# Where buffers lie and where small sums run in an attention and feed-forward kernel: a change of placement in the second half

## The chip, the cores and the metric

The kernel runs on one core of one Trainium2 chip. The metric is the device time of one execution in microseconds (us). The kernel before takes 2131.32 us, the median of three runs (2130.99 to 2131.37).

A core has a matrix engine (PE; its weight loads are listed apart as PEld), a vector engine (DVE), an activation engine (ACT), GpSimd (POOL) and a queue (SP) that issues most of the DMAs. Each engine works through its own list in the order in which the program gives it. PE writes to PSUM; DVE and ACT read PSUM; POOL works on SBUF alone.

## The reference

Eight sequences of 512 rows and 512 columns pass through attention and then a feed-forward block. Everything is in fp32.

```python
x = x + layernorm(attention(layernorm(x)))          # 16 heads of 32, rotary on all of q and k
h = layernorm(x)
h = fwht(h * SU_ug) / SCALE                          # Walsh-Hadamard over 512
up   = h @ W_up.T   * (Wscale_ug[:2048] * SCALE)     # 512 -> 2048
gate = h @ W_gate.T * (Wscale_ug[2048:] * SCALE)
h = fwht(silu(gate) * up * SU_dp) / SCALE            # Walsh-Hadamard over 2048
h = h @ W_down.T * (Wscale_dp * SCALE)               # 2048 -> 512
out = x + layernorm(h)
```

## The kernel before

**Two halves.** Up to about 916 us the program does attention for the eight sequences and stores the rows of `x + layernorm(attention)` to DRAM (`x1d`). From there on it does the feed-forward block. The change is in the second half alone.

**The end of attention.** The last sequence's four tiles of 128 rows are normed by DVE (line 955), added to the input rows by POOL (956) and stored by DMAs that POOL issues (957). They lie in four buffers `y` of the attention's pools. The feed-forward pools `fw` and `fs` are laid over the attention's pools. A tile tag gets its place when it is first asked for, in that order: `tt_room` and `pr_room` at lines 1053 and 1054 fix the places of `tt` (8 buffers of 3584 bytes in each partition) and `pr` (6 of 4096); then come `sig` and the `g` tiles. The first writer of a tile waits for the last users of what lay there.

**Pairs and features.** The sequences are taken in four pairs p (bA = 2p, bB = 2p + 1). The 2048 features are 16 blocks of 128; i runs over 8, and block i goes with block i + 8. For one i, the 2 x 2 problem (two feature blocks, two halves of the input columns, two sequences) is done by Strassen's scheme: seven products in the order 1, 2, 6, 5, 7, 3, 4, on sums of weights and of operands, joined by additions.

**The first pair** (p = 0, to about 1180 us; `seven`, line 1149): each i has a gate unit ("g") and an up unit ("u"), so 16 units u = 0 to 15. A product is two matmuls over 512 columns, in one of four PSUM buffers that go round (`ubank`). Product 1 is copied to SBUF by ACT (m1); DVE adds it to product 2 (c11, line 1170), to product 6 (u2, 1172), then 7, 3 and 4; ACT copies product 5 (m5, 1174); POOL makes c22 and c12 (1177, 1180). `catch_up` runs three scalings or activations of the unit before. `middle` runs the input steps below, `filler` runs down matmuls. `hook(n)` is called after the step of product n. Weights' sums over two blocks of the first pair's unit are made by POOL for the next unit at a unit's start (`combine`, 144) and, over gate and up, by DVE into four tiles w2 (`deep_weights`, lines 1018 to 1021); `deep_keep` writes all to DRAM for the later pairs. `load_unit` loads weights two units ahead.

**The deep pairs** (p = 1, 2, 3; `pair`, line 1311, and `deep`, 1098): gate and up are joined by a second Strassen level. Each of the seven products n is now seven small products m in the order 1, 2, 6, 5, 7, 3, 4 over 256 columns, each in one `ubank`. ACT copies small products 1 (line 1115) and 5 (1119), DVE does the five additions 1116, 1118, 1122, 1124 and 1127, POOL two (1123, 1125) and the additions between products (1320). After m = 2, 5 and 3 `deep` calls `place(1)`, `place(2)` and `place(3)`, and `copied` after the copy of small product 5: other work is hung in there, named (n, at). `part()` runs one down matmul (two instructions of 512 columns).

**The operands of a pair** are sums of quarters of the Hadamard-transformed inputs `xb`: `operand` (T1 to T4, line 230, 1024 columns), `deep_operand` (three sums of 256 columns for each n into a `tt` tile, line 1005), and `deep_last` (one in place, line 1010, needed by small product 7 of that n). `prepare` (line 1279) has a table of which is made at which (i, n, at).

**Input steps.** Each 128-row tile of the next pair is loaded (`in_load`), its statistics taken (`in_stats`: DVE and two small POOL instructions), its shift made (`in_shift`, DVE), normed (`in_norm`, ACT), transposed (`in_flip`) and Hadamard-transformed (`in_had`). `FIRST_CUTS` and `CUTS` say how many steps run in each unit or i.

**Down and end.** Each finished feature block `g` (`scale`, line 1143) is multiplied with four column blocks of the down weights (line 1205) into four PSUM banks. After 16 blocks `finish` scales the four banks into `fy` (1230) and hangs the ends on a list: statistics of four tiles (`norms`), a shift, and `close`, which norms by ACT (1252), adds the residual by POOL and stores. `proceed` runs the next end. All orders are written out by hand (manual schedule).

Of the kernel before, what the change touches and what calls it, by code (L numbers as in the profile page):

```python
# [10 lines left out]
F32 = mybir.dt.float32  # L11
BF16 = mybir.dt.bfloat16
I32 = mybir.dt.int32
AF = mybir.ActivationFunctionType
# [19 lines left out]
def sandwich_kernel(  # L34
# [952 lines left out]
    def tt_tile(name):  # L987
        return fs.tile([P, 7 * P], F32, tag="tt", name=name, bufs=8)
# [1 line left out]
    def pr_tile(name):  # L990
        return fs.tile([P, 2, S], F32, tag="pr", name=name, bufs=6)

    def deep_operand(p, n, k=None):

        if k in (None, 0):
            if n == 4:
                t = xb[2 * p + 1][:, 0:2].rearrange("p k s -> p (k s)")
            else:
                t = tt_tile(f"tt{n}_{p}")
            tt[p, n] = t[:, : 3 * HS].rearrange("p (a s) -> p a s", a=3)  # L1000
        x_, t = ops[p][OPERAND[n]], tt[p, n]
        a, b = [
            (x_[:, 0, HS:], x_[:, 0, :HS]), (x_[:, 1, HS:], t[:, 0]), (x_[:, 1, :HS], t[:, 1]),
        ][k]
        nc.vector.tensor_sub(t[:, k], a, b)
# [6 lines left out]
    def deep_weights(i):  # L1012

        w2[i] = t0, t1, t2, t3 = [
            tt_tile(f"w2_{i}_{k}").rearrange("p (s m) -> p s m", m=P) for k in range(4)
        ]
        wg, wu = wt[0, i, "g"][:, 0:7], wt[0, i, "u"][:, 0:7]
        nc.vector.tensor_add(t0, wu[:, :, 0], wu[:, :, 1])
        nc.vector.tensor_sub(t1, t0, wg[:, :, 0])
        nc.vector.tensor_sub(t2, wg[:, :, 1], t1)  # L1020
        nc.vector.tensor_sub(t3, wg[:, :, 0], wu[:, :, 0])


    INNER = {1: 0, 2: 1, 5: 2, 6: 3, 3: 4, 7: 5, 4: 6}
# [26 lines left out]


    tt_tile("tt_room")
    pr_tile("pr_room")
    psy0 = [ps_y.tile([P, D], F32, tag=f"y{t}", name=f"psy_0_{t}") for t in range(NT)]
    ubank("u0")
# [92 lines left out]
    def seven(p, i, what, filler, middle, hook):  # L1149

        def use(c, b, half):
            f = i + half * NH
            if what == "g":
                gs[b, f] = fs.tile([P, S], F32, tag="sig", name=f"s_{b}_{f}", bufs=4)
                activate(gs[b, f], c, f)
            else:
                scale(b, f, c, gs.pop((b, f)))

        def catch_up():
            while late:
                late.pop(0)()

        bA, bB = 2 * p, 2 * p + 1
        t = [pr_tile(f"pr{what}{k}_{i}") for k in range(4)]
        m1, m5, u2, c11 = t[0][:, 0], t[0][:, 1], t[1][:, 0], t[1][:, 1]
        u3, c22, c12 = t[2][:, 0], t[2][:, 1], t[3][:, 0]
        nc.scalar.copy(m1, product(p, i, what, 1))
        nc.vector.tensor_add(c11, product(p, i, what, 2), m1)  # L1170
        catch_up()
        nc.vector.tensor_add(u2, product(p, i, what, 6), m1)
        use(c11, bA, 0)
        nc.scalar.copy(m5, product(p, i, what, 5))
        hook(5)
        nc.vector.tensor_add(u3, product(p, i, what, 7), u2)
        nc.gpsimd.tensor_add(c22, u3, m5)
        hook(7)
        nc.vector.tensor_add(c12, product(p, i, what, 3), u2)
        nc.gpsimd.tensor_add(c12, c12, m5)  # L1180
        hook(3)
        middle()
        filler()
        nc.vector.tensor_add(u3, product(p, i, what, 4), u3)
        late.extend([lambda: use(c22, bB, 1), lambda: use(c12, bB, 0), lambda: use(u3, bA, 1)])

    psy = {}
# [37 lines left out]
    def finish(b, t, ps):  # L1225
# [15 lines left out]
        def norms(t):  # L1241
            bn(mv[:, t, :], y[:, t], f"o{b}_{t}")
            if t == NT - 1:
                sr.append(inverse_std(mv, NT, f"o{b}"))
                residuals(0)

        def close(t):
            if t == 0:
                sr.append(shift_of(mv, sr[0], NT, f"o{b}"))
            rs, sh = sr  # L1250
            for t in (t, t + 1):
                nc.scalar.activation(
                    y[:, t], y[:, t], AF.Identity, bias=sh[:, t : t + 1], scale=rs[:, t : t + 1]
                )
                nc.gpsimd.tensor_add(y[:, t], r[t], y[:, t])
                nc.sync.dma_start(out=out[b, ts(t, P), :], in_=y[:, t])
            if t == 1:
                residuals(2)

        for t in range(NT):  # L1260
            ends.append(lambda t=t: norms(t))
        for t in (0, 2):
            ends.append(lambda t=t: close(t))

    def proceed():
        if ends:
            ends.pop(0)()

    queue = []

# [8 lines left out]
    def prepare(p, i, n, at):  # L1279
        q = p + 1 if i >= NH - 2 else p  # L1280
        if q >= NP or q == 0:
            return
        todo = {
            (NH - 2, 7, 1): [("ops",), ("tt", 1, 0)], (NH - 2, 7, 2): [("tt", 1, 1)],
            (NH - 2, 7, 3): [("tt", 1, 2)], (NH - 2, 3, 1): [("tt", 2, 0)],
            (NH - 2, 3, 2): [("tt", 2, 1)], (NH - 2, 3, 3): [("tt", 2, 2)],
            (NH - 1, 7, 1): [("T", 0)], (NH - 1, 7, 2): [("T", 1)], (NH - 1, 7, 3): [("last", 1)],
            (NH - 1, 3, 1): [("T", 2)], (NH - 1, 3, 2): [("tt", 6, 0), ("tt", 6, 1)],
            (NH - 1, 3, 3): [("tt", 6, 2)], (NH - 1, 4, 1): [("tt", 5, 0), ("tt", 5, 1)],
            (NH - 1, 4, 2): [("tt", 5, 2), ("tt", 7, 0)], (NH - 1, 4, 3): [("tt", 7, 1), ("tt", 7, 2)],  # L1290
            (0, 1, 1): [("T", 3)], (0, 1, 2): [("last", 2)], (0, 1, 3): [("last", 6)],
            (0, 2, 1): [("tt", 3, 0)], (0, 2, 3): [("tt", 3, 1), ("last", 5)],
            (0, 6, 1): [("tt", 3, 2), ("last", 7)], (0, 6, 2): [("tt", 4, 0)],
            (0, 6, 3): [("tt", 4, 1)], (0, 5, 1): [("tt", 4, 2)], (0, 5, 2): [("last", 3)],
            (0, 5, 3): [("last", 4)],
        }
        for kind, *which in todo.get((i, n, at), ()):
            if kind == "ops":
                ops[q] = {"B11": xb[2 * q][:, 0:2], "B21": xb[2 * q][:, 2:4], "B22": xb[2 * q + 1][:, 2:4]}
            elif kind == "tt":  # L1300
                deep_operand(q, *which)
            elif kind == "T":
                operand(q, *which)
            else:
                deep_last(q, *which)


    PARTS = {1: (1, 3), 2: (1, 3), 6: (1, 2, 3), 5: (1, 3), 7: (1, 3), 3: (1, 2, 3), 4: (1, 3)}
# [2 lines left out]
    def pair(p, i, inputs):  # L1311
# [16 lines left out]
        def copied(n):  # L1328

            if n in (1, 2, 6) and before:  # L1330
                silu(*before[{1: "c22", 2: "c12", 6: "c21"}[n]])
            elif n == 5:
                silu(pr[2], bA, i)

        def place(n, at):
            if at in PARTS[n]:
                part()
            key = n, at
            if late and n in (1, 2) and at == 2:
                while late:  # L1340
                    late.pop(0)()
            elif before and key in ((2, 2), (6, 3), (5, 1)):
                end(*before[{2: "c22", 6: "c12", 5: "c21"}[n]])
            elif key in ((6, 1), (6, 2)):
                nc.vector.tensor_add(pr[2][:, at - 1], pr[2][:, at - 1], pr[1][:, at - 1])
            elif key == (7, 1):
                end(pr[2], bA, i)
            prepare(p, i, n, at)

        for n in ORDER:  # L1350
            now[0] += 1
# [2 lines left out]
                load_two(q // 2 + 2)  # L1354
            if n in (2, 5, 3):
                if inputs:
                    in_step(*inputs.pop(0))
                proceed()
            pr[n] = pr_tile(f"pr{n}_{p}_{i}")
            deep(  # L1360
                p, i, n, pr[n][:, 0], pr[n][:, 1], lambda n=n: copied(n), lambda at, n=n: place(n, at)
            )
            if n == 6:
                add(6, 6, 1)
            elif n == 7:
                add(7, 7, 6)
# [7 lines left out]

    CUTS = [0, 3, 6, 9, 12, 14, 16, 16, 16]
    FIRST_CUTS = [0, 0, 0, 1, 2, 3, 5, 6, 7, 9, 10, 11, 13, 14, 15, 16, 16]
    first = 2 * NT
    for _ in range(3):  # L1380
        wd_load()
    for u, (p, i, what) in enumerate(units):
# [9 lines left out]
            deep_keep(i, what)  # L1392
        steps = [(2 * NT + s // 2, s % 2, len(rows)) for s in range(FIRST_CUTS[u], FIRST_CUTS[u + 1])]

        def middle():
            if u == 1:
                deep_weights(0)
                in_stats(first)
                in_stats(first + 1)
            while steps:  # L1400
                in_step(*steps.pop(0))
            proceed()
            if what == "g" and i > 0:
                deep_weights(i)

        def filler():
            if u >= 2 * NH - 2:
                for at in (1, 2, 3):
                    prepare(0, NH - 2 + u % 2, 3, at)
            down()  # L1410

        def hook(n):
            if u >= 2 * NH - 2 and n == 7:
                for at in (1, 2, 3):
                    prepare(0, NH - 2 + u % 2, 7, at)

        seven(p, i, what, filler, middle, hook)
        if u == 1:
            deep_keep(0, what)
            in_shift(first)  # L1420
            in_shift(first + 1)
            in_norm(first)
        if u == 2 * NH - 1:
            for at in (1, 2, 3):
                prepare(0, NH - 1, 4, at)
        down()
    for p in range(1, NP):
        for i in range(NH):
# [121 lines left out]
```

## Time and profile before

| | |
|---|---|
| median of three runs | 2131.32 us |
| the profiled execution's own time | 2132.84 us |
| its span, first to last instruction | 2131.1 us |
| PE busy | 2087.3 us, 98% |
| DVE, ACT, POOL busy | 1408.7, 744.2, 1567.0 us |
| PE clock granted | 0.995 of full speed |
| DMA | 218 MB, a mean of 102 GB/s |

A profile line of a group or of the timeline names the source line, the engine, the operation, what it writes and reads, its shape and its count; in square brackets stands the idle time of its engine before it and what ended that. A busy PE is not a PE at its peak: the end of a matmul is modelled, so the rate is better read from one start to the next. An fp32 matmul shows as two instructions.

### The profile page before, as it was taken

To read this page: it belongs to the slowest core of one execution; us is meant where nothing else is said; L and a number is where in the kernel's file an instruction comes from. 1 tells how busy PE (TensorE), PEld (TensorE's weight loads), DVE (VectorE), ACT (ScalarE), POOL (GpSimd) and SP (SyncE) were. 2 spreads that over 40 slices of the span, in tenths; PEclk is the share of its full clock that TensorE was granted. 3 is DMA by queue.
4 is the path that set the end of the run, shared out by engine and by line. 5 is a ranking of instruction groups with operands and counts; after the bars stand their busy time and mean duration, and the time that the engine had idled before them with its cause. 6 is when DMAs were issued, how large, how long until landed. Compare 5 with 4: busy or idle time off the path is not lost.

```text
span 2131.1 us, 26822 instructions
## 1 busy us (share of the span) xinstructions
PE 2087.3 (98%) x9035; PEld 1056.8 (50%) x9042; DVE 1408.7 (66%) x2362; ACT 744.2 (35%) x1199; POOL 1567.0 (74%) x1623
## 2 busy tenths in 40 slices
PE   8999999999999999989999999999999999999998
PEld 4333333333333333334444667766666776777663
DVE  5697877676767677355556866668756569556542
ACT  3554545454555555512111132222222221222211
POOL 4787979697978788545554578788787787787862
PEclk9999999999999999999999999999999999999999
DMA  3112121212121122317454444443343343443331
GB/s 120 36 31 51 45 56 41 61 41 55 46 48 54 26 70 74 111 47 220 146 169 151 143 149 138 127 156 122 117 151 125 118 171 123 149 156 132 135 114 69
DMA packets 215914, 218.13 MB, mean 102 GB/s; under 512 B 87376, under 2 KB 147920, under 8 KB 215776
## 3 DMA queue, kind: packets, MB, share of 16 engines
q1 hardware_dynamic: 215424, 215.32, 32.4%
q8 instruction: 72, 1.18, 0.2%
q0 software_dynamic: 352, 1.08, 0.1%
q14 instruction: 66, 0.54, 0.1%
HBM read 169.18 MB, written 46.92 MB: 101 GB/s over the span
## 4 chain that ended last, share of the span: by engine, by line
PE 89%; DVE 6%; issue 2%; POOL 1%; ACT 1%; DMA 0%; POOLq 0%; SPq 0%; DVEq 0%; ACTq 0%
PE d L1108 21%; PE psy L1205 16%; PE s L520 6%; PE ops L599 6%; PE ps_k L432 5%; PE ps_y L655 5%; PE t L566 5%; PE u L1093 4%; PE g L1093 4%; PE psz L1451 3%; PE t L557 2%; PE l L616 2%; PE ps_q L447 1%; PE ps_v L459 1%; PE ps_cq L400 1%
## 5 line engine op out<-in xcount | busy, mean ns | idle before, releaser
L1205 PE MATMUL psy<-wd,g 128*128 128x512 f32 x896 | 449.8, 593 | 0.0
L528 DVE TENSOR_REDUCE nm<-s 128x2 f32<-128x1024 f32 x256 | 300.8, 1217 | 176.5 <-PE s L520 176.4
L1320 POOL TENSOR_TENSOR pr<-pr,pr 128x512 f32<-128x512 f32 x288 | 368.6, 1307 | 7.5
L587 POOL TENSOR_TENSOR p<-p,p 128x512 f32<-128x512 f32 x244 | 329.8, 1382 | 22.2 <-PE ops L599 22.2
L578 ACT ACTIVATE p<-t 128x1024 f32<-128x1024 f32 x256 | 251.8, 1023 | 89.2 <-PE t L566 89.2
L1123 POOL TENSOR_TENSOR pr<-db 128x256 f32<-128x256 f32 x168 | 127.4, 759 | 172.8 <-DVE db L1122 147.4
L1108 PE MATMUL d<-tt,wq 128*128 128x256 f32 x864 | 235.8, 381 | 2.4 <-DVE pr L1127 1.5
L1108 PEld LDWEIGHTS d<-tt,wq 128*128 128x128 f32 x864 | 163.5, 190 | 149.5 <-issue 102.4
L1108 PE MATMUL d<-T,wq 128*128 128x256 f32 x768 | 199.4, 381 | 4.5 <-ACT da L1115 1.8
L1205 PEld LDWEIGHTS psy<-wd,g 128*128 128x128 f32 x896 | 169.9, 190 | 48.4 <-issue 28.7
L1108 PE MATMUL d<-xb,wq 128*128 128x256 f32 x720 | 185.1, 381 | 5.5 <-DVE db L1122 2.3
L1119 ACT COPY db<-d 128x256 f32<-128x256 f32 x168 | 62.5, 372 | 308.9 <-PE d L1108 250.5
L1115 ACT COPY da<-d 128x256 f32<-128x256 f32 x168 | 62.3, 371 | 303.4 <-PE d L1108 182.1
L1108 PEld LDWEIGHTS d<-xb,wq 128*128 128x128 f32 x720 | 134.7, 190 | 61.8 <-issue 31.6
L1108 PEld LDWEIGHTS d<-T,wq 128*128 128x128 f32 x768 | 144.1, 190 | 42.2 <-issue 12.7
L520 PE MATMUL s<-kT,qT 32*128 32x512 f32 x1024 | 153.8, 639 | 0.7 <-DVE nm L528 0.7
L566 PE MATMUL t<-qT,kT 32*128 32x512 f32 x1024 | 142.8, 598 | 0.0
L1125 POOL TENSOR_TENSOR pr<-pr,db 128x256 f32<-128x256 f32 x168 | 138.1, 822 | 0.0
L599 PE MATMUL ops<-p,v 128*32 128x512 f32 x1024 | 136.8, 605 | 0.0
L1127 DVE TENSOR_TENSOR pr<-d,db 128x256 f32<-128x256 f32 x168 | 70.7, 421 | 89.0 <-PE d L1108 88.2
L432 PE MATMUL ps_k<-xT,wkr_sb 128*128 128x512 f32 x256 | 118.3, 605 | 0.7 <-ACT xT L390 0.7
L655 PE MATMUL ps_y<-wo_sb,oT 128*128 128x512 f32 x256 | 115.8, 593 | 0.9 <-DVE oT L650 0.6
(206 smaller groups left out, 3243.9 us busy)
## 6 DMA issues: line engine op xcount, KB each, us to landing
wq<-wdeep SPq DMA_DIRECT2D x168, 448.0 KB, 4.2
wd<-wdd SPq DMA_DIRECT2D x112, 256.0 KB, 2.6
wdeep<-w SPq DMA_DIRECT2D x32, 448.0 KB, 5.7
xr<-in_x SPq DMA_DIRECT2D x32, 256.0 KB, 2.7
xin<-x1d SPq DMA_DIRECT2D x32, 256.0 KB, 2.9
xres<-x1d SPq DMA_DIRECT2D x32, 256.0 KB, 3.2
out<-fy SPq DMA_DIRECT2D x32, 256.0 KB, 2.0
rec<-rd SPq DMA_DIRECT2D x124, 64.0 KB, 2.0
```

The source lines that it names most:

```text
L432: nc.tensor.matmul(ps, lhsT=wkr_sb[:, k, ts(g, P)], rhs=xT[b][:, k, :], start=(k == 0), stop=(k == NK - 1),)
L520: nc.tensor.matmul(sp[j // 2][:, j % 2, :], lhsT=qT[b][rows, g, ts(qc, P)], rhs=kT[b][rows, g, :], start=True, stop=True,)
L528: nc.vector.tensor_reduce(nms[n][:, qc, 2 * h : 2 * h + 2], sp[h], AX.X, ALU.max, negate=True)
L566: nc.tensor.matmul(sp[j // 2][:, j % 2, :], lhsT=kT[b][rows, g, ts(c, P)], rhs=qT[b][rows, g, :], start=False, stop=True,)
L578: nc.scalar.activation(pt[n, c, h], sp[h], AF.Exp)
L587: nc.gpsimd.tensor_add(into, into, pt[n, c, j // 2][:, j % 2, :])
L599: nc.tensor.matmul(o_ps[n][j * DH : (j + 1) * DH, :], lhsT=vv[b][:, c, ds(g * P + j * DH, DH)], rhs=pt[n, c, j // 2][:, j % 2, :], start=( ...
L655: nc.tensor.matmul(ps, lhsT=oT[b][:, k, ts(qc, P)], rhs=wo_sb[:, k, :], start=False, stop=(k == NK - 1),)
L1093: nc.tensor.matmul(ps, lhsT=w[:, SLOT[n], k, :], rhs=rhs[:, k, :], start=k == 0, stop=k == 1)
L1108: nc.tensor.matmul(ps, lhsT=w[:, INNER[m]], rhs=rhs[m], start=True, stop=True)
L1205: nc.tensor.matmul(ys_[t], lhsT=g[:, ts(t, P)], rhs=w, start=n == 0, stop=n == NI - 1)
L1320: nc.gpsimd.tensor_add(pr[n][:, h], pr[a][:, h], pr[b][:, h])
```

## The change

- Twelve tiles `g0` to `g11` are asked for between `tt_room` and `pr_room`, so that `g` takes the place where `pr` was, and `pr` and `sig` lie further on.
- `deep_weights` returns its four sums as a list; the unit loop runs one at each hook but the first (2, 5, 7, 3), in unit 1 and in each later gate unit. Before, they ran together in `middle`.
- The statistics of the second pair's first two rows move from unit 1 to unit 2, the first steps one unit later (`FIRST_CUTS`); in the deep pairs the steps begin at i = 1 and not at i = 0 (`CUTS`). In the deep pairs statistics and shifts run at place 3 of the product, the norm at `copied`.
- The ends are marked "vector" or "scalar". Vector ones run at places (1, 2), (7, 2), (4, 2), scalar ones at `copied` of products 7 and 4. The shift becomes an end of its own, and `close` does one tile and not two.
- `prepare`'s table: the first two operands of the next pair move from products 7 and 3 to 1, 2 and 3 at i = 6; operands for 5 and 7 move from i = 7 to i = 0; those for 3 and 4 move later within i = 0. For p = 1 the first part is done in unit 15's hooks.
- At i = 0 of a deep pair the two additions into `pr[2]` go from DVE to POOL. Late scalings run one at a place.

```diff
@@ deep_weights
-        nc.vector.tensor_add(t0, wu[:, :, 0], wu[:, :, 1])
-        nc.vector.tensor_sub(t1, t0, wg[:, :, 0])
...
+        return [
+            lambda: nc.vector.tensor_add(t0, wu[:, :, 0], wu[:, :, 1]),
+            lambda: nc.vector.tensor_sub(t1, t0, wg[:, :, 0]),
...
     tt_tile("tt_room")
+    for n in range(12):
+        fs.tile([P, S], F32, tag=f"g{n}", name=f"g{n}_room")
     pr_tile("pr_room")
@@ seven
         nc.scalar.copy(m1, product(p, i, what, 1))
+        hook(1)
         nc.vector.tensor_add(c11, product(p, i, what, 2), m1)
+        hook(2)
         catch_up()
...
         nc.vector.tensor_add(u3, product(p, i, what, 4), u3)
+        hook(4)
@@ finish
+        def shift():
+            sr.append(shift_of(mv, sr[0], NT, f"o{b}"))
         def close(t):
-            if t == 0:
-                sr.append(shift_of(mv, sr[0], NT, f"o{b}"))
             rs, sh = sr
-            for t in (t, t + 1):
-                nc.scalar.activation(
...
+            nc.scalar.activation(
...
         for t in range(NT):
-            ends.append(lambda t=t: norms(t))
-        for t in (0, 2):
-            ends.append(lambda t=t: close(t))
-    def proceed():
-        if ends:
-            ends.pop(0)()
+            ends.append(("vector", lambda t=t: norms(t)))
+        ends.append(("vector", shift))
+        for t in range(NT):
+            ends.append(("scalar", lambda t=t: close(t)))
+    def proceed(by=None):
+        if ends and by in (None, ends[0][0]):
+            ends.pop(0)[1]()
@@ prepare
-            (NH - 2, 7, 1): [("ops",), ("tt", 1, 0)], (NH - 2, 7, 2): [("tt", 1, 1)],
-            (NH - 2, 7, 3): [("tt", 1, 2)], (NH - 2, 3, 1): [("tt", 2, 0)],
+            (NH - 2, 1, 2): [("ops",), ("tt", 1, 0)], (NH - 2, 1, 3): [("tt", 1, 1)],
+            (NH - 2, 2, 3): [("tt", 1, 2)], (NH - 2, 3, 1): [("tt", 2, 0)],
             (NH - 2, 3, 2): [("tt", 2, 1)], (NH - 2, 3, 3): [("tt", 2, 2)],
-            (NH - 1, 7, 1): [("T", 0)], (NH - 1, 7, 2): [("T", 1)], (NH - 1, 7, 3): [("last", 1)],
-            (NH - 1, 3, 1): [("T", 2)], (NH - 1, 3, 2): [("tt", 6, 0), ("tt", 6, 1)],
-            (NH - 1, 3, 3): [("tt", 6, 2)], (NH - 1, 4, 1): [("tt", 5, 0), ("tt", 5, 1)],
-            (NH - 1, 4, 2): [("tt", 5, 2), ("tt", 7, 0)], (NH - 1, 4, 3): [("tt", 7, 1), ("tt", 7, 2)],
+            (NH - 1, 7, 2): [("T", 0)], (NH - 1, 7, 3): [("T", 1)], (NH - 1, 3, 1): [("last", 1)],
+            (NH - 1, 3, 2): [("T", 2)], (NH - 1, 4, 1): [("tt", 6, 0)],
+            (NH - 1, 4, 2): [("tt", 6, 1)], (NH - 1, 4, 3): [("tt", 6, 2)],
             (0, 1, 1): [("T", 3)], (0, 1, 2): [("last", 2)], (0, 1, 3): [("last", 6)],
-            (0, 2, 1): [("tt", 3, 0)], (0, 2, 3): [("tt", 3, 1), ("last", 5)],
-            (0, 6, 1): [("tt", 3, 2), ("last", 7)], (0, 6, 2): [("tt", 4, 0)],
-            (0, 6, 3): [("tt", 4, 1)], (0, 5, 1): [("tt", 4, 2)], (0, 5, 2): [("last", 3)],
-            (0, 5, 3): [("last", 4)],
+            (0, 2, 1): [("tt", 5, 0)], (0, 2, 3): [("tt", 5, 1)], (0, 6, 1): [("tt", 5, 2)],
+            (0, 6, 2): [("last", 5), ("tt", 7, 0)], (0, 5, 1): [("tt", 7, 1)],
+            (0, 5, 2): [("tt", 7, 2)], (0, 5, 3): [("last", 7)], (0, 7, 1): [("tt", 3, 0)],
+            (0, 7, 2): [("tt", 3, 1)], (0, 7, 3): [("tt", 3, 2)], (0, 3, 1): [("last", 3)],
+            (0, 3, 2): [("tt", 4, 0)], (0, 3, 3): [("tt", 4, 1)], (0, 4, 1): [("tt", 4, 2)],
+            (0, 4, 2): [("last", 4)],
@@ pair
+            elif n in (7, 4):
+                proceed("scalar")
...
-            if late and n in (1, 2) and at == 2:
-                while late:
-                    late.pop(0)()
+            if late and key in ((1, 2), (2, 2), (2, 3)):
+                late.pop(0)()
...
-            elif key in ((6, 1), (6, 2)):
+            elif key in ((6, 1), (6, 2)) and i > 0:
                 nc.vector.tensor_add(pr[2][:, at - 1], pr[2][:, at - 1], pr[1][:, at - 1])
             elif key == (7, 1):
                 end(pr[2], bA, i)
+            elif key in ((1, 2), (7, 2), (4, 2)):
+                proceed("vector")
+            for fn in after.pop(key, ()):
+                fn()
             prepare(p, i, n, at)
...
+        def step(n, j, had, last):
+            if had:
+                in_had(j)
+                if j + 2 < last:
+                    after[n, 3] = [lambda: in_shift(j + 2)]
+                if j + 1 < last:
+                    after[n, 0] = [lambda: in_norm(j + 1)]
+                return
+            in_flip(j)
+            if j + 3 < last:
+                in_load(j + 3)
+            if j + 2 < last:
+                after[n, 3] = [lambda: in_stats(j + 2)]
...
-                    in_step(*inputs.pop(0))
-                proceed()
+                    step(n, *inputs.pop(0))
...
-            if n == 6:
+            if n == 2 and i == 0:
+                add(2, 2, 1)
+            elif n == 6:
                 add(6, 6, 1)
@@ cuts and units
-    CUTS = [0, 3, 6, 9, 12, 14, 16, 16, 16]
-    FIRST_CUTS = [0, 0, 0, 1, 2, 3, 5, 6, 7, 9, 10, 11, 13, 14, 15, 16, 16]
+    CUTS = [0, 0, 3, 6, 9, 12, 14, 16, 16]
+    FIRST_CUTS = [0, 0, 0, 0, 1, 2, 4, 5, 7, 8, 10, 11, 13, 14, 15, 16, 16]
...
+        if what == "g" and i > 0 or u == 1:
+            sums = deep_weights(i)
...
         def hook(n):
-            if u >= 2 * NH - 2 and n == 7:
-                for at in (1, 2, 3):
-                    prepare(0, NH - 2 + u % 2, 7, at)
+            if sums and n != 1:
+                sums.pop(0)()
+            if u == 2 and n in (1, 2):
+                in_stats(first + n - 1)
+            if u == 2 * NH - 1:
+                for kind in {
+                    1: [("ops",), ("tt", 1)], 2: [("tt", 2)], 5: [("T", 0)], 7: [("T", 1), ("last", 1)],
+                    3: [("T", 2)], 4: [("tt", 6)],
+                }[n]:
+                    make(1, *kind)
```

## The prediction

> **What bounds the kernel now.** The page gives TensorE 2087 of 2131 us, so only its gaps can be won. I looked first at the busy times by stretch from 916 us on, where the second half of the program starts, and cut the stretches around the idle places (columns: length, then busy time and count of PE, PEld, DVE, ACT and POOL, PE clock, DMA):
>
> ```profile
> 916.00:938.00 22.00, 13.75 (x28) 5.78 (x27) 10.29 (x21) 4.46 (x7) 11.77 (x17) 0.77 0.12 48
> 954.00:960.00 6.00, 4.25 (x10) 1.63 (x9) 4.57 (x9) 1.18 (x2) 1.51 (x5) 1.00 0.47 139
> 1180.00:1208.00 28.00, 26.02 (x88) 16.56 (x87) 27.66 (x58) 5.05 (x12) 11.92 (x15) 0.94 0.35 108
> 1264.00:1270.00 6.00, 4.72 (x20) 3.18 (x19) 4.05 (x8) 2.67 (x5) 5.92 (x8) 1.00 0.18 44
> 1460.00:1504.00 44.00, 38.70 (x140) 24.68 (x139) 41.59 (x78) 10.16 (x23) 34.97 (x33) 1.00 0.35 121
> 1570.00:1577.00 7.00, 5.20 (x20) 3.48 (x19) 4.30 (x9) 3.04 (x6) 6.92 (x8) 1.00 0.00 0
> 1765.00:1799.00 34.00, 31.44 (x112) 20.22 (x111) 33.90 (x59) 6.95 (x16) 29.17 (x24) 1.00 0.38 125
> 1799.00:2050.00 251.00, 250.82 (x934) 176.94 (x933) 146.99 (x321) 60.30 (x137) 196.28 (x199) 1.00 0.41 140
> ```
>
> The last row shows the floor: nothing is lost there. A steady matmul instruction takes 0.43 us from start to start for 512 columns and 0.215 for 256. Summed that way (a busy PE at half clock, or with a modelled end, hides some loss), the stretches lose 10.9, 2.0, 5.0, 1.5, 8.6, 2.1 and 4.3 us, 34.4 in all. Check on 1460:1504: by the groups, 28 x 0.43 + 106 x 0.215 + 4 transposes x 0.11 = 35.3 of 44.
>
> The timeline tells what ends the three kinds of wait. First, the start of the first pair:
>
> ```profile
> 922.18 2.85 DVE L955 TENSOR_SCALAR y<-y,rs_y,sh_y 128x512 f32<-128x512 f32 x4
> ...
> 928.99 0.56 POOL L957 DMA_DIRECT2D x1d<-y  x1 [0.30 <-POOL y L956]
> ...
> 931.41 0.58 ACT L1169 COPY prg<-g 128x512 f32<-128x512 f32 x1 [13.37 <-DMA x1d<-y]
> ...
> 932.05 3.78 PE L1093 MATMUL g<-T,w_g 128*128 128x512 f32 x4 [8.25 <-ACT prg L1169]
> ```
>
> The copy of the first product waits until attention's third row store has landed, because its `pr` tile lies on the `y` rows. PE fills its four PSUM banks and stops for 8.4 us; the next six instructions then run at 0.85 instead of 0.43 us.
>
> Second, the deep pairs' close, which puts ACT behind DVE:
>
> ```profile
> 1265.85 0.54 DVE L114 SCALAR_TENSOR_TENSOR sh_o<-mvo,rs_o 128x4 f32<-128x4 f32 x1
> ...
> 1266.42 1.52 ACT L1252 ACTIVATE fy<-fy,sh_o,rs_o 128x512 f32<-128x512 f32 x2 [2.82 <-DVE sh_o L114]
> ...
> 1267.85 0.35 ACT L1115 COPY da<-d 128x256 f32<-128x256 f32 x1
> ...
> 1268.25 1.13 PE L1108 MATMUL d<-xb,wq 128*128 128x256 f32 x4 [1.28 <-ACT da L1115]
> ```
>
> Third, where one pair passes to the next, a DVE without gaps holds PSUM banks:
>
> ```profile
> 1774.54 0.94 DVE L1005 TENSOR_TENSOR tt<-T 128x256 f32<-128x256 f32 x1
> 1775.40 0.41 DVE L1122 TENSOR_TENSOR db<-d,da 128x256 f32<-128x256 f32 x1
> 1775.74 0.41 DVE L1124 TENSOR_TENSOR pr<-d,da 128x256 f32<-128x256 f32 x1
> 1775.87 0.70 PE L1108 MATMUL d<-xb,wq 128*128 128x256 f32 x2 [1.14 <-DVE db L1122]
> ```
>
> **The Trainium skill.** "TensorE: Matmul & The Clock Gate", Part 1, says that an idle window of about 3.4 us halves PE's clock until a window of activity has passed: the trace agrees (0.85 us per instruction after the 8.4 us gap, 0.43 from 937 on). The same page, Part 2, lets PE pull weight loads ahead, while ACT and DVE are strict FIFO: so a late DVE instruction delays all behind it, as the second excerpt shows. "SBUF — State Buffer", Who interferes with whom: a DVE instruction with two SBUF inputs and a GpSimd one that reads SBUF exclude each other. The trace agrees: L1005 takes 0.41 us alone and 0.94 above, beside POOL; its 63 average 0.82, L1010's 21 0.64.
>
> **The change part by part.**
>
> *Twelve `g` tiles reserved ahead of `pr`.* In the built program before, `pr` covers bytes 137120 to 161696 of a partition and the `y` rows 134688 to 142880. Twelve `g` of 2048 bytes move `pr` up by 24576, wholly onto the weights tiles of the last softmax groups, which PE last reads at 909.0. So the copy can run at 918.5, when product 1 is out. What is late next: DVE reaches L1170 after L955 at 925.03, and frees product 2's bank at 925.8; PE wants it at 923.64 + 1.72 = 925.36. I leave 0.45 us and no clock loss: gain 10.9 - 0.45 = **10.4**. On POOL, L1177 queues behind the row stores until 931.7; only ACT's later activations wait for it (until about 934.2, before the copy of product 5 at 936). The wait moves to the first `g`: unit 1 now starts at 929.2 and writes it near 935, after the stores under it have landed (931.3). The tile under the fourth store (w2's second) is written near 936; that store is issued at 931.14 and at 2.3 us lands at 933.5. Both hidden by 2 to 4 us; without cover each microsecond late is one lost.
>
> *Weights' sums one by one, statistics a unit later.* The second row is DVE's block L1018 to L1021 (950.81 to 956.08) plus two statistics (1.7 us) ahead of the L1184 for which PE waits. Spread over four hooks, 1.1 us each: gain **2.0**. In later g units L1018 now waits on DVE right after c11, 3.4 us into the unit, for POOL's combine, which ends 0.5 to 1.1 us into it (986.5 for 986.0, 1019.7 for 1018.7). In unit 2 the load starts only when L1021 is done (941.5 now), lands 3.8 us later (as from 956.15 to 959.95), and POOL needs 2.9: DVE is held from 945 to 948.3, then 1.1 + 0.9 + 3 x 0.7 + 0.7 brings product 6's add to 953.1; PE first does eight down instructions until 954.9. Hidden by 1.8 us. SP's order of loads keeps its place behind the same sums.
>
> *Closes split, shift in a DVE place of its own, one activation at a time.* Removes the ACT waits: gain 1.5 + 2.1 = **3.6**. Norms (0.66 + 0.18 us), statistics and shifts now sit inside a product, where four banks cover them; on ACT an activation of 0.8 us follows the fifth small product's copy, and the next copy is due 2 us later. On SP the input loads move with their steps, the residual loads and the stores come one close at a time: a block's nine ends, three of DVE's and two of ACT's per i, finish by the fourth i, and `fy` is written again in the fifth, about 9 us later. Cover gone, `fy`'s first row would hold DVE.
>
> *Operands of the next pair later and evenly, no input steps at i = 0, the two adds of pr2 there on POOL.* Per pair: the first two operands move to i = 6, seven to two blocks: i = 7 loses six L1005 and carries 35 x 0.335 (back to back) + 3 x 1.34 + 4 x 0.82 + 4 x 1.0 + 1.2 = 24 us on DVE in 34.9 of PE: no wait left. At i = 0 DVE has 11.7 + 1.3 + 12 x 0.82 + 6 x 0.64 + 4 x 1.0 + four y rows 2.4 + two norms 1.7 = 34.8 of 34.9: full. Stepping through it with four banks I find waits of 0.35 and 0.75 (product 5, after three y rows), 0.5 (product 3), and a new one: `last 4` is placed at (4, 2), behind a norm, and PE's seventh small product needs it: 0.42 + 0.84 + 0.5 + 0.1 after small 6, less 0.43 of PE's own, 1.5 us (behind it on DVE are the product's last three adds, for which PE's next product waits). Left over 3.1 per pair. POOL's extra 2 x 1.31 fits its 3.1 us gap at 1788; ACT's Silu of pr2 waits for it, two products later. So 8.6 becomes 3.1 (gain **5.5**) and 4.3 becomes 3.1 (**1.2**). Into the first deep pair, three late `g` (0.7 each) come on top: about 4.0 of 5.0 stays (**1.0**).
>
> Sum: 10.4 + 2.0 + 3.6 + 5.5 + 1.2 + 1.0 = 23.7 us. The profiled execution took 2132.84 (span 2131.1 and 1.7 around it), 1.5 over the median of 2131.32; I take the sum from the median: **2107.6**.
>
> **Unknown ends.** No trace shows how often the moved SBUF sums meet POOL. At 0.41 each nothing is lost at i = 0 but the 1.5; at 0.94 (the second excerpt of L1005) 18 (12 L1005 and 6 L1010) cost 2.6 more, and scales up to 1.34 another 1.4: 3.1 becomes 7. I take the mean.
>
> **The rivals.**
> - *The first wait is only handed on* (the `g` tiles or the w2 under the stores hold DVE, and PE, as long): no 10.4, so 2118. For: the same bytes are still waited for. Against: the 2 to 4 us above. 0.10.
> - *Just-in-time operands make DVE the bound at i = 0*: 7 lost in each of three passages instead of 3 to 4, so 2107.6 + 11 = 2119. For: 34.8 of 34.9. 0.15.
> - *All hidden*: also the 0.45 and 4.0 + 3.1 + 3.1 go: 2097. Against: `last 4`. 0.12.
> - *Slower*: L1018, now early in DVE's queue, stands for POOL's combine in all eight g units. Its slack is until 6.4 us into the unit (u2 must free a bank by 10.3); to eat 23.7 us, eight units must lose 3.0 each, so the combine would have to end 9.4 us into the unit, not 1.1; at 10 us the time would be 2136. For: POOL's queue holds the input steps' sums and powers ahead of it. Against: the three ends above. 0.03.
>
> **The numbers.** My forecast has 0.60. 2098 to 2119 leaves out most of *all hidden* and the upper part of the second rival. Two tenths of a per cent (4 us) is about what can be told from no change; all cases but the last are faster by more: faster 0.95, same 0.02, slower 0.03.
>
> **What would show it.** Right: no wait of L1093 on L1169 near 923; clock 1.00 there; L1170 at about 925; no 5 us DVE block near 951; no ACT wait before L1115; at each i = 0 a wait of about 1.5 us on DVE's L1010 in the last product. Wrong: PE waits for L1143 or L1018 in the first pair, or DVE-held banks of over 5 us per passage.

## The result, and the profile after

The changed kernel takes 2121.56 us (median of 5 runs, 2117.10 to 2123.64) where the kernel before takes 2131.37 beside it: a ratio of 0.9947, with a 95% interval of 0.9932 to 0.9962. By the medians that is 9.8 us. The forecast was 23.7 us, and its range, 2098 to 2119, ends below the measured median. The profiled execution took 2117.10 us (span 2115.3); it is the fastest of the five, 4.5 us below their median, and the table below explains this one execution, not those 4.5 us. Its span is 15.8 us shorter than before, and 1.9 of that lies in attention, which the change doesn't touch: the first product of the second half starts at 914.8 instead of 916.8. In the trace before, PE's clock is at half for some 3.4 us near 29 us, which is enough for about 1.7 of it; in the trace after it is not.

The same view as before, busy time by stretch, now around the places where the changed kernel loses (columns: length, busy time and count of PE, PEld, DVE, ACT and POOL, PE clock, DMA):

```profile
916.00:938.00 22.00, 21.74 (x51) 9.42 (x50) 15.85 (x28) 6.40 (x10) 16.93 (x22) 1.00 0.12 48
996.00:1002.00 6.00, 4.89 (x15) 2.31 (x14) 3.44 (x8) 0.37 (x1) 3.81 (x5) 1.00 0.38 118
1168.00:1210.00 42.00, 39.51 (x146) 27.05 (x145) 36.79 (x73) 6.52 (x18) 27.25 (x28) 1.00 0.36 119
1264.00:1270.00 6.00, 6.00 (x23) 4.18 (x22) 3.84 (x9) 1.46 (x3) 3.13 (x6) 1.00 0.47 156
1460.00:1504.00 44.00, 38.81 (x135) 25.52 (x135) 36.14 (x71) 8.93 (x21) 42.69 (x39) 0.96 0.31 108
1762.00:1796.00 34.00, 30.04 (x107) 19.66 (x107) 29.09 (x57) 5.96 (x14) 32.85 (x30) 1.00 0.53 178
```

The start of the first pair and the close at 1264 are full. The passage at 1460 is as empty as before, but with DVE at 36 us instead of 42 and POOL at 43 instead of 35. A place that was full is now not: 996. Counted from start to start, as in the prediction, the losses from 916 us on are (us; the forecast's column is what it left):

| place | before | forecast | after |
|---|---|---|---|
| start of the first pair | 10.9 | 0.45 | 0.5 |
| sums of weights, 954 | 2.0 | 0 | 0 |
| closes: 1264, 1570 and small ones | 5.4 | 1.8 | 0.2 |
| passage 0 to 1 | 5.0 | 4.0 | 3.2 |
| passage 1 to 2 | 8.6 | 3.1 | 9.5 |
| passage 2 to 3 | 4.3 | 3.1 | 5.2 |
| units at 998 and 1065 | 0 | 0 | 2.7 |
| loads of the last weights, 2050 | 0 | 0 | 1.1 |
| all | 36.2 | 12.5 | 22.3 |

So this execution gained 13.9 us in the second half and not 23.7. Of the 9.8 that are missing, 7.7 lie in the three passages (17.9 instead of 10.2), 3.8 in two places that the forecast put at nothing; the closes gained 1.6 more than forecast.

The timeline at the start of the first pair: ACT's copy (L1173, before L1169) no longer waits, and of 8.4 us 0.3 is left, behind DVE's four `y` rows, as forecast.

```profile
916.75 0.59 ACT L1173 COPY prg<-g 128x512 f32<-128x512 f32 x1 [0.64 <-PE g L1097]
...
920.24 2.86 DVE L955 TENSOR_SCALAR y<-y,rs_y,sh_y 128x512 f32<-128x512 f32 x4
...
923.84 1.96 PE L1097 MATMUL g<-xb,w_g 128*128 128x512 f32 x4 [0.26 <-DVE prg L1175]
```

At a close, the activation now stands behind a copy that PE waits for, not ahead of it, and waits for nothing:

```profile
1278.62 0.37 ACT L1123 COPY db<-d 128x256 f32<-128x256 f32 x1 [1.86 <-PE d L1112]
1278.89 0.81 ACT L1259 ACTIVATE fy<-fy,sh_o,rs_o 128x512 f32<-128x512 f32 x1
```

Passage 1 to 2 opens with a wait that was not there before. In the timeline POOL adds a residual row for a close (L1262) and is late with L1129; ACT's copy L1123 needs the tile that L1129 reads; PE needs the bank that L1123 empties:

```profile
1468.46 1.27 POOL L1262 TENSOR_TENSOR fy<-xres,fy 128x512 f32<-128x512 f32 x1
...
1470.56 1.16 POOL L1129 TENSOR_TENSOR pr<-pr,db 128x256 f32<-128x256 f32 x1
...
1471.76 0.37 ACT L1123 COPY db<-d 128x256 f32<-128x256 f32 x1 [4.45 <-POOL pr L1129]
...
1472.18 1.13 PE L1112 MATMUL d<-T,wq 128*128 128x256 f32 x4 [0.98 <-ACT db L1123]
```

From there PE runs small products only: between 1470.2 and 1483.4 it has no down product (L1212), and it loses 0.28 to 1.69 us at five places where DVE is late. The down products on both sides of it, and the longest of the five waits:

```profile
1469.75 1.02 PE L1212 MATMUL psy<-wd,g 128*128 128x512 f32 x2
...
1481.99 0.70 PE L1112 MATMUL d<-T,wq 128*128 128x256 f32 x2 [1.53 <-DVE da L1122]
...
1483.39 1.47 PE L1212 MATMUL psy<-wd,g 128*128 128x512 f32 x2
```

At the end of i = 0 comes the forecast wait for `last 4`, with two statistics ahead of it on DVE:

```profile
1497.98 0.68 DVE L99 BATCH_NORM_STATS2 st_o<-fy 128x6 f32<-128x512 f32 x1
...
1498.70 0.18 DVE L100 BATCH_NORM_AGGREGATE mvo<-st_o 128x2 f32<-128x6 f32 x1
1498.80 0.47 DVE L1010 TENSOR_TENSOR T<-T 128x256 f32<-128x256 f32 x1
...
1499.41 1.10 PE L1112 MATMUL d<-T,wq 128*128 128x256 f32 x4 [1.38 <-DVE T L1010]
```

The new place at 998: a unit that has both steps of one row sends the transform (L204) straight after the flip, and PE waits for DVE's copy of it, behind an addition for the product:

```profile
997.59 0.69 DVE L1185 TENSOR_TENSOR pru<-u,pru 128x512 f32<-128x512 f32 x1 [1.09 <-PE u L1097]
998.20 0.68 DVE L197 TENSOR_TENSOR xflat<-fxt,su 128x512 f32<-128x512 f32 x1
...
999.02 1.10 PE L204 MATMUL fxh<-xflat,h 128*128 128x512 f32 x2 [1.11 <-DVE xflat L197]
```

And near the end the loads of the last eight weights stand on SP behind the last store of a close, which waited for its POOL addition until 2045.2:

```profile
2045.22 0.34 SPq L1263 DMA_DIRECT2D out<-fy  x1
2045.60 3.76 SPq L1084 DMA_DIRECT2D wdl<-wdd  x8
...
2050.93 1.55 PE L1490 MATMUL psz<-wdl,g 128*128 128x512 f32 x3 [0.47 <-DMA wdl<-wdd]
```

### The profile page after: what moved, and what is told of

It reads as the page before. It is cut to its first block, busy times and chain, and to the rows that moved or that the text cites. A ratio compares the mean times of both kernels' runs of the same rounds, so it can differ in the third digit from the quotient of the medians.

```text
span 2115.3 us, 26783 instructions
## 1 busy us (share of the span) xinstructions
PE 2081.0 (98%) x9042; PEld 1057.5 (50%) x9042; DVE 1408.2 (67%) x2356; ACT 745.3 (35%) x1199; POOL 1573.5 (74%) x1629
## 4 chain that ended last, share of the span: by engine, by line
PE 90%; DVE 4%; POOL 3%; issue 1%; ACT 1%; DMA 1%; SPq 0%; POOLq 0%; DVEq 0%; ACTq 0%
PE d L1112 22%; PE psy L1212 17%; PE s L520 6%; PE ops L599 6%; PE ps_k L432 5%; PE ps_y L655 5%; PE t L566 5%; PE u L1097 4%; PE g L1097 4%; PE t L557 3%; PE psz L1490 2%; PE l L616 2%; POOL pr L1334 2%; PE ps_q L447 1%; PE ps_v L459 1%; PE ps_cq L400 1%
## 5 line engine op out<-in xcount | busy, mean ns | idle before, releaser
L1212 PE MATMUL psy<-wd,g 128*128 128x512 f32 x896 | 449.3, 593 | 0.0
L1334 POOL TENSOR_TENSOR pr<-pr,pr 128x512 f32<-128x512 f32 x294 | 381.1, 1324 | 7.4
L1127 POOL TENSOR_TENSOR pr<-db 128x256 f32<-128x256 f32 x168 | 132.2, 787 | 115.7 <-DVE db L1126 104.2
L1212 PEld LDWEIGHTS psy<-wd,g 128*128 128x128 f32 x896 | 169.8, 190 | 49.3 <-issue 29.4
L1123 ACT COPY db<-d 128x256 f32<-128x256 f32 x168 | 62.7, 373 | 323.5 <-PE d L1112 266.1
L1129 POOL TENSOR_TENSOR pr<-pr,db 128x256 f32<-128x256 f32 x168 | 137.4, 818 | 0.0
```

The costliest lines, as they stand in the source:

```text
L1212: nc.tensor.matmul(ys_[t], lhsT=g[:, ts(t, P)], rhs=w, start=n == 0, stop=n == NI - 1)
L1334: nc.gpsimd.tensor_add(pr[n][:, h], pr[a][:, h], pr[b][:, h])
```

## The experiments

My theory after these traces: the rooms are nearly the whole gain; by the losses above, the rest of the change wins some 9 us (2.0 at the sums, 5.2 at the closes, 1.8 in passage 0 to 1) and gives 5.6 of it back, at five places with four causes. All times are medians of 4 runs or more; ratios are to the kernel before, run beside each. "Lost" is counted in each run's own trace from the start of the second half on, with the passages in their order. In some traces PE runs at half clock for a stretch of about 3.4 us after a wait (last section). This adds about 1.7 us to passage 0 to 1 of e3, e7 and e10 and to passage 1 to 2 of e3; in passages where PE would have waited anyhow, such a stretch adds next to nothing.

| kernel | us | ratio (95%) | lost | passages |
|---|---|---|---|---|
| before, first pair of runs | 2131.37 | | 36.2 | 5.0, 8.6, 4.3 |
| changed, once more (e5) | 2119.68 | 0.9946 (0.9929 to 0.9962) | 21.9 | 3.2, 9.5, 5.2 |
| e1 rooms alone | 2120.75 | 0.9947 (0.9932 to 0.9962) | 25.5 | 5.0, 8.6, 4.3 |
| e2 rooms out | 2130.54 | 0.9993 (0.9984 to 1.0001) | 32.3 | 3.1, 9.4, 5.1 |
| e3 two-step units | 2116.37 | 0.9929 (0.9914 to 0.9944) | 23.8 | 4.9, 11.2, 5.2 |
| e4 passage undone | 2121.46 | 0.9950 (0.9934 to 0.9967) | 25.4 | 5.0, 10.1, 5.8 |
| e6 last sooner | 2111.91 | 0.9905 (0.9890 to 0.9919) | 15.9 | 1.4, 7.4, 3.1 |
| e7 closes sooner | 2114.25 | 0.9917 (0.9902 to 0.9932) | 20.2 | 4.9, 8.1, 3.9 |
| e8 parts held | 2111.28 | 0.9901 (0.9886 to 0.9916) | 15.1 | 3.2, 4.0, 4.0 |
| e9 four together | 2100.50 | 0.9855 (0.9841 to 0.9870) | 5.0 | 1.4, 1.2, 1.2 |
| e10 additions on DVE | 2124.18 | 0.9962 (0.9948 to 0.9976) | 27.1 | 5.0, 11.1, 6.8 |
| e11 rooms, parts held | 2116.51 | 0.9930 (0.9915 to 0.9945) | 21.2 | 5.0, 4.2, 4.3 |

**Rooms alone (on the kernel before), and rooms out (of the changed one).**

```diff
     tt_tile("tt_room")
+    for n in range(12):
+        fs.tile([P, S], F32, tag=f"g{n}", name=f"g{n}_room")
     pr_tile("pr_room")
```

> The kernel before plus the twelve rooms g0 to g11 and nothing else of the change. Theory (the rooms are nearly all of what the change gained, the rest of it gives as much as it takes): the copy L1169 no longer waits for the third row store, the 10.9 us lost at 916 to 938 fall to 0.5, every later place stays as before, so 10.4 us less than before, about 2121 us, the same time as the whole change. Rival (the rooms give less than the trace says, because the eight waits they remove are handed on to the next copy or to the first use of wsu): 2126 us or more, with a new wait of several us between 920 and 940.

> The changed kernel with the twelve rooms taken out. Theory: the first feature blocks fall back on the buffers that the last rows leave from, the wait on the third row store and the clock at one half behind it return, 10 to 11 us more than the changed kernel, so level with the kernel before within 3 us (about 2130). Rival (the other parts of the change gain some 5 us by themselves, as forecast): 2124 to 2127.

Both theories hold, both rivals fall. The rooms alone give the ratio of the whole change, and without them the change can't be told from the kernel before. Busy time by stretch, rooms alone and then rooms out:

```profile
916.00:938.00 22.00, 21.73 (x51) 9.42 (x50) 13.08 (x26) 6.88 (x11) 16.89 (x23) 1.00 0.12 48
```

```profile
916.00:938.00 22.00, 13.73 (x27) 5.69 (x27) 10.04 (x21) 4.14 (x6) 11.96 (x18) 0.77 0.12 48
```

Rooms alone still lose 1.7 us where DVE makes the sums of weights in a block (now at 945), and 5.5 at the closes, so in the traces those two parts of the change win what they were to win; neither was taken out alone.

**Two-step units.**

```diff
-    FIRST_CUTS = [0, 0, 0, 0, 1, 2, 4, 5, 7, 8, 10, 11, 13, 14, 15, 16, 16]
+    FIRST_CUTS = [0, 0, 0, 0, 1, 3, 4, 5, 7, 8, 9, 11, 12, 13, 15, 16, 16]
```

> The changed kernel with FIRST_CUTS 0,0,0,0,1,3,4,5,7,8,9,11,12,13,15,16,16, so that each unit with two input steps has the transform of one row and the flip of the next, never flip and transform of one row. Theory: the two waits of L204 on the copy xflat (1.27 us each at 998 and 1065) go, nothing else moves: 2.5 us less lost between 940 and 1160. Rival (the wait only moves to another unit, since the same number of steps runs in the same time): the sum over 940 to 1160 stays within 0.5 us.

The loss between 962 and 1160 goes from 2.7 to 0.0: shown. In the unit at 998 the transform no longer waits:

```profile
998.23 1.02 PE L204 MATMUL fxh<-xflat,h 128*128 128x512 f32 x2
```

The passages of this profiled run lose 3.4 more than those of the changed kernel, nearly all of it in products at half clock behind the same waits (last section); its other runs took 2115.3 to 2116.8.

**The passage part undone, and only its two additions.**

```diff
         todo = {
-            (NH - 2, 1, 2): [("ops",), ("tt", 1, 0)], (NH - 2, 1, 3): [("tt", 1, 1)],
...
+            (NH - 2, 7, 1): [("ops",), ("tt", 1, 0)], (NH - 2, 7, 2): [("tt", 1, 1)],
...
-            elif key in ((6, 1), (6, 2)) and i > 0:
+            elif key in ((6, 1), (6, 2)):
...
-            if n == 2 and i == 0:
-                add(2, 2, 1)
-            elif n == 6:
+            if n == 6:
```

The last two hunks alone are the kernel with the additions on VectorE.

> The changed kernel with the operands of the next pair made where the kernel before makes them (its table, its calls in the last two units of the first pair, the first product's two additions at i=0 on VectorE again); rooms, sums of weights, input steps and ends of rows stay changed. Theory (the passage part gained nothing in sum: 17.9 us are lost in the three passages of the kernel before, 17.9 in the three of the changed one): the passages lose 16 to 20 us and the time is within 2 us of the changed kernel. Rival (the passage part did gain, and the later ends of rows on GpSimd took it back): without it the passages lose 5 us or more above 17.9, and the kernel is 5 us or more slower than the changed one.

> The changed kernel with the first product's addition at i=0 on VectorE again (two of 128x512 at product 6, places 1 and 2, as the kernel before has it) instead of on GpSimd after product 2. Theory (in i=0 VectorE is what TensorE waits for, and two additions of some 0.65 us each matter there): 1 to 3 us more lost in the passages than in the changed kernel, most of it at 1473 to 1483. Rival (GpSimd's queue is what stretches VectorE's instructions and holds the sig tiles): the passages lose 1 us or more less, since L1010 is no longer slowed beside GpSimd's additions.

Without the passage part the passages lose 20.9 us instead of 17.9, just above the theory's range and well below the rival's: the part wins 3.0, not the 7.7 forecast, and in time this can't be told. With only the additions back on DVE they lose 22.9, 5.0 more. Some 1.7 of that are products at half clock in passage 0 to 1; the rest, about 3.3, is just above the 1 to 3 that I expected, and the intervals of the two ratios overlap. So GpSimd's load is not a reason against moving the additions. What the later operands do by themselves can't be told: with the additions on DVE, they lose 2.0 more than the table of before, about what the half clock takes.

**Last differences sooner.**

```diff
-            (0, 7, 2): [("tt", 3, 1)], (0, 7, 3): [("tt", 3, 2)], (0, 3, 1): [("last", 3)],
-            (0, 3, 2): [("tt", 4, 0)], (0, 3, 3): [("tt", 4, 1)], (0, 4, 1): [("tt", 4, 2)],
-            (0, 4, 2): [("last", 4)],
+            (0, 7, 2): [("tt", 3, 1)], (0, 7, 3): [("last", 3)], (0, 3, 1): [("tt", 3, 2)],
+            (0, 3, 2): [("tt", 4, 0)], (0, 3, 3): [("tt", 4, 1)], (0, 4, 1): [("last", 4)],
+            (0, 4, 2): [("tt", 4, 2)],
```

> The changed kernel with two pairs of VectorE instructions of i=0 exchanged: the last difference of products 3 and 4 is issued one place ahead of the third tt of the same product, which TensorE needs only at that product's end. Theory (the order in VectorE's queue costs it: TensorE reaches the fifth matmul of the product before the difference is made): the waits on L1010 at 1202, 1492, 1498, 1786 and 1792 (2.35, 0.67, 1.54, 1.45, 1.54; 7.6 us) fall to 2.5 us or less, 5 us or more less in the passages. Rival (VectorE is full there, whatever the order): the waits come back at L1010's neighbours and the passages lose within 2 us of what the changed kernel's lose.

With its base beside it (e5) it is 7.8 us faster, and it loses 6.0 less in the passages. Of the five waits, 7.6 us, there remain 0.33 and 0.33 on L1010 and 0.54 on the L1005 that changed places with it; two new ones of 0.52 are for DVE's L1126. That is 2.2 us in all. The timeline of DVE and PE at the last product of passage 1 to 2: the same two statistics now stand behind L1010 and not ahead of it.

```profile
1494.70 0.82 DVE L1010 TENSOR_TENSOR T<-T 128x256 f32<-128x256 f32 x1
1495.45 0.41 DVE L1122 TENSOR_TENSOR da<-d,da 128x256 f32<-128x256 f32 x1
1495.79 0.68 DVE L99 BATCH_NORM_STATS2 st_o<-fy 128x6 f32<-128x512 f32 x1
```

```profile
1495.67 1.10 PE L1112 MATMUL d<-T,wq 128*128 128x256 f32 x4 [0.16 <-DVE T L1010]
```

DVE does the same work in the same i. What cost these 6.0 us was its order, not how much work it has.

**Ends of rows sooner.**

```diff
-            elif n in (7, 4):
+            elif n in (7, 3, 4):
                 proceed("scalar")
```

> The changed kernel with the ends of rows taken at products 7, 3 and 4 instead of 7 and 4, so that the fourth residual addition of a block comes about half an i earlier. Theory (the fourth addition, 1.27 us on GpSimd at product 4 of i=7, is what delays L1129 and with it the copy L1123, and its out store stands ahead of the loads of the last weights): the two waits of 1.14 us at 1471 and 1765 and the 1.07 us at 2050 go, 3.3 us less lost. Rival (GpSimd's queue is behind by the six additions after product 7 alone): the two waits stay at 0.8 us or more and only the 1.07 us go.

The rival falls: both waits of about 1.14 us and the loss at 2050 are gone. It is 5.4 us faster than its base. ACT's copy now comes in time, and PE goes on without a wait, at the place of the wait at 1471:

```profile
1471.74 0.91 POOL L1129 TENSOR_TENSOR pr<-pr,db 128x256 f32<-128x256 f32 x1
...
1472.69 0.37 ACT L1123 COPY db<-d 128x256 f32<-128x256 f32 x1 [2.78 <-POOL pr L1129]
1473.21 0.59 PE L1112 MATMUL d<-tt,wq 128*128 128x256 f32 x2
1473.64 1.03 PE L1112 MATMUL d<-T,wq 128*128 128x256 f32 x4
```

In its profiled run passage 0 to 1 lost 1.7 more, at half clock.

**Down products held, on the changed kernel and on rooms alone.**

```diff
-            if at in PARTS[n]:
+            if at in PARTS[n] and not (p == 1 and i >= 2 and (n, at) == (6, 2)):
                 part()
```

> The changed kernel with one matmul of the down product left for later in each i from 2 on of the second pair (the one at product 6, place 2), six in all, which then run when the third pair begins. Theory (in passage 1 to 2 TensorE waits on VectorE because it has no down product for 13.2 us, 1470.2 to 1483.4): the stretch without L1212 shrinks to 4 us or less, and the passage loses 4 to 6.5 us instead of 9.5. Rival (VectorE's own work in that stretch is too long whatever TensorE does meanwhile, or the held parts leave i=2 to 7 short): the passage loses 8.5 us or more, or the i before it lose what it gains.

> The kernel before with the twelve rooms and with the six down matmuls of the second pair held for the third, and none of the change's other parts. Theory (the 8.6 us that the kernel before loses in its passage 1 to 2 are not a matter of where the operands stand in VectorE's queue, but of TensorE having no down product there for 14.1 us): the passage loses 3 to 5 us, and the time is 3.5 us or more below that of the rooms alone, 2117 us or less. Rival (the order of the operands makes that loss, as the prediction had it): the passage still loses 7 us or more.

The longest stretch in the passage without a down product falls from 13.2 to 4.3 us (just above the 4 expected), and the passage's loss from 9.5 to 4.0. Part of the backlog is handed on: passage 2 to 3 loses 1.2 less too. The six held parts are 12 matmul instructions of 0.43, 5.2 us of PE work; the loss in this passage fell by 5.5. On the table of before, the same six parts take passage 1 to 2 from 8.6 to 4.2. Busy time from 1470 to 1484 in the changed kernel, and from 1465 to 1485 with held parts:

```profile
1470.00:1484.00 14.00, 10.68 (x38) 6.27 (x37) 12.56 (x26) 4.20 (x9) 13.76 (x13) 0.99 0.69 245
```

```profile
1465.00:1485.00 20.00, 19.02 (x70) 12.77 (x69) 18.39 (x37) 4.84 (x11) 19.69 (x19) 1.00 0.55 191
```

DVE is busy 90 to 92% of both stretches. PE is busy 76% of the first and 95% of the second: with held parts it has work of its own meanwhile.

**The changed kernel once more, and the four edits together.**

> The changed kernel once more, unaltered, as the base on the same chip for the three runs beside it: 2117 to 2124 us, about 22 us lost from 916 on in its trace, of it 3.2, 9.5 and 5.2 in the three passages.

> The changed kernel with the four edits of the runs before together: two-step units that take the transform of one row and the flip of the next, the last differences of products 3 and 4 one place sooner, ends of rows at products 7, 3 and 4, and six down matmuls of the second pair held for the start of the third. Theory (the four losses are separate: 2.7 in the units, about 7 on L1010, 3.4 behind GpSimd and the late close, 5 in the stretch without down products): 22 us lost become 4 to 7, and the time is 2099 to 2104 us. Rival (they stand in for one another: VectorE full in i=0 is the one bound): 10 us or more are still lost, 2107 us or more.

The four add up: 22.3 less 2.7, 6.0, 3.4 and 6.7 by the runs above would leave 3.5, and 5.0 are left. At 2100.5 us it beats both kernels. Its trace for the stretch of passage 1 to 2:

```profile
1460.00:1504.00 44.00, 43.34 (x163) 29.98 (x162) 38.00 (x79) 10.05 (x23) 39.37 (x39) 1.00 0.33 115
```

## Why the prediction was right and wrong

- *Twelve `g` tiles reserved*: right, mechanism and size (10.9 to 0.5, forecast 0.45; by rooms alone about 11 us in time). The rival "the first wait is only handed on" is out.
- *Weights' sums one by one*: right by the traces, 2.0 to 0. DVE does wait for POOL's combine, until 947.8 (forecast 948.3), and PE loses nothing there. The rival "slower" had no part in it.
- *Closes split*: the gain was right and undersized (5.2, not 3.6; I had counted two of its places). The step that failed is its cost, "finish by the fourth i". I took the freedom of `fy` as the limit and named no other work behind these ends. The addition on POOL and the store on SP move with each activation, to i = 7: this cost the waits of 1.14 us in the last two passages and 1.1 us at 2050, shown by taking the ends sooner. (The prediction's second excerpt shows an order kept on ACT, where a copy stands behind an activation that waits, not one kept on DVE, as its text has it.)
- *Input steps*: the same part of the prediction has "the input loads move with their steps" and gives the new cuts no cost. Two units got flip and transform of one row, 2.7 us, shown by other cuts.
- *Operands of the next pair*: this is the step on which the forecast failed, "Left over 3.1 per pair". 10.2 were to be left in the three passages, and 17.9 are. Its balance of "34.8 of 34.9: full" has on PE's side all the down products of an i. They aren't there at i = 0 of the third pair: the last block of b = 2 is scaled only at place (5, 1) of that i, b = 3 waits its turn behind it, and all earlier blocks are used up. So for 13.2 us PE has no down product to put beside DVE's work, and 5.2 us of held down products took 5.5 off that passage's 9.5. The kernel before has the same gap (14.1 us without its down product, L1205, in that passage). I read its 8.6 us there as DVE's operands only; rooms with held parts show that 4.4 of it is this. Against the forecast, passage 1 to 2 lost 6.4 more, of which the held parts take away 5.5; passage 2 to 3 lost 2.1 more, where the late closes (1.3 by e7) and the wait for `last 3` (1.45) are what was not forecast; passage 0 to 1 lost 0.8 less.
- *`last 4`*: the mechanism was right and the size half right: 1.54 twice, as forecast, but 2.35 in passage 0 to 1, where L1010 takes 1.27 us beside POOL's additions. `last 3` does the same (0.67 and 1.45), which I had not seen.
- *Unknown ends*: the rival "just-in-time operands make DVE the bound" gave 2119, near the result, but for another reason. It has these instructions at 0.94 us or more; L1005 and L1010 took 0.79 each on average. Its sum has a slip too: from the means that the prediction uses, 0.82 and 0.64, 12 and 6 instructions at 0.94 cost 3.2 us more, not 2.6, so that the rival's time would be about 2120.5. And with the same DVE work, a better order, cover by down products and a shorter GpSimd queue brought 17.9 down to 3.8.
- *The range*: the median missed 2098 to 2119 by 2.6 us. That it came so near is luck: the upper end was the rival's, whose reason is not the one found. No case in it let two mis-sized terms come together, and the 3.8 us for the units and the tail were in none. Not tested alone: starting the deep pairs' input steps at i = 1, and their new places within a product.

## What to carry to other kernels

Before an engine is called full in a stretch, count what the engine that waits for it has to do there by itself; work that can be held back for such a stretch can be worth about its own length (here 5.2 us of it took off 5.5 in one kernel and 4.4 in the other). When a step is moved, follow every queue that it is put on to what stands behind it there: here the activation on ACT was free, and the addition on POOL and the store on SP that go with it cost 3.4 us. Within a product, issue first what is needed first: two exchanges won 6.0 us in the passages, the whole table of new places and moved additions 3.0.

## What the runs showed of the hardware

The same wait is followed by full clock in one execution and by half in another. This holds for one and the same program: in passage 1 to 2 of the changed kernel's profiled run the clock is at half from 1484 to 1487 (first line), and in the run of the unaltered kernel once more (e5), with the same waits before it, it is at full speed throughout (second line). Here the half clock cost next to nothing: both executions lose 9.5 us in the passage, and PE's wait for `last 3` behind it is 0.67 us in the first and 1.45 in the second.

```profile
1484.00:1487.00 3.00, 3.00 (x8) 2.04 (x7) 2.23 (x4) 0.03 (x1) 3.00 (x4) 0.50 0.10 38
```

```profile
1460.00:1504.00 44.00, 37.63 (x138) 24.71 (x137) 37.46 (x71) 9.26 (x21) 42.77 (x38) 1.00 0.31 108
```

Where PE has work afterwards, it costs. In the changed kernel's profiled run the wait for `last 4` at 1202 left the clock at 1.00; in the run with other two-step units, the down products behind the same wait ran at 0.85 instead of 0.43 us (timeline of PE, the changed kernel and then the other):

```profile
1204.60 1.10 PE L1112 MATMUL d<-T,wq 128*128 128x256 f32 x4 [2.18 <-DVE T L1010]
1205.54 1.02 PE L1212 MATMUL psy<-wd,g 128*128 128x512 f32 x2
```

```profile
1202.41 1.88 PE L1112 MATMUL d<-T,wq 128*128 128x256 f32 x4 [2.19 <-DVE T L1010]
1204.08 1.91 PE L1212 MATMUL psy<-wd,g 128*128 128x512 f32 x2
```

It lasts about 3 us (clock 0.50 from 1203 to 1206) and costs 1.7. The idle time was 2.2 us, less than the idle window of some 3.4 that the Trainium skill gives in "TensorE: Matmul & The Clock Gate", Part 1. The page has the window run freely, and that the outcome differs between runs fits this; that one wait of 2.2 us comes before the halving does not follow from its idle window, and what decides it stays open. The changed kernel's runs lie 6.5 us apart; I take the half clock for the cause, since their mean clock falls from 0.998 to 0.996 with the time, but only profiled runs show where, so this is not shown. Nor can it be told from the waits alone: with the four edits the longest wait in the passages is 0.54 and the runs lie 2.3 us apart, but those of the kernel with held parts, which has waits of 2.35 and 1.90 us, lie only 2.6 apart.
